# When ScalarE scales du * B: another division of its pieces over the steps of a selective scan

## The chip, the cores and the metric

The kernel runs on one core of a Trainium2 chip, in one launch. The metric is the device time of that launch in microseconds (us), the median of several runs. In what follows TensorE is PE in the profile, VectorE is DVE, ScalarE is ACT, GpSimd is POOL, and SP is the queue that issues the DMAs.

## What is computed

The reference is a small network in four layers on an image of shape 4 x 64 x 64 x 96. Layers 0 and 1 are state-space blocks (projection, depthwise convolution, SiLU, a selective scan in four directions, a normalisation, a gate and a projection; layer 1 works between a Fourier transform and its inverse). Layers 2 and 3 are attention and feed-forward layers. Nearly all of the time goes to the selective scans. For each direction, channel d and state n of 16:

```python
dA = jnp.exp(dl[..., None] * A)
hst = hst * dA + (dl * ul)[..., None] * bl[:, :, None, :]
y = jnp.einsum('bkdn,bkn->bkd', hst, cl)
```

`dl` is delta, a softplus of a projection; `ul` is the input; `bl` and `cl` are the B and C of that time step. The product `du = dl * ul` times `bl` is the "du * B" of this document.

## The kernel before

**Segments and steps.** The scans are cut into segments of up to 512 time steps. Block l0 (layer 0) has two image pairs, four directions and eight segments of 512: 64 segments, with two images side by side on the partitions (`NI` is 2). Block l1 (layer 1) has four images, four directions and segments of 512, 512, 384, 384 and 320: 80 segments, `NI` is 1. A segment is worked off in 12 steps: four quarters q of the 16 states, and in each of them three chunks c of 128 channels. A step (q, c) handles four states of one chunk. The steps run (0,0), (0,1), (0,2), (1,0) and so on to (3,2); there are 1728 of them.

**One step.** VectorE runs four scan instructions (line 643): two for the first two states (the tile hx), two for the others (hy), and then one multiply with C (line 807, the tile hcy). Each scan needs its exp(delta * A), made by ScalarE (line 618), and its du * B:

- For the hx pair, du * B is made on ScalarE in time-major layout, in `make_bx` (line 593), and transposed by TensorE into PSUM (line 613). One call of `make_bx` makes the two states of a quarter for all three chunks. It consists of 16 pieces in l0 (two states, four blocks of 128 time steps, two images; 128x192 each), and in l1 of 8 pieces for 512 time steps or 6 for 384 and 320 (128x384 each). It is a generator: each `next` issues one piece. This document calls the 6 to 16 pieces of one call a set.
- For the hy pair, du * B is made by GpSimd (line 636). Only the exp stands in PSUM.

The exps of the hy pair and the transposed hx products share a ring of three PSUM buffers (the tag `ab`; in the trace the names ab, b and a shortened _l). So an exp can be written only after the scan that used the buffer before has ended. ScalarE's order in a step is: exp of the fourth scan (`front_y(st, 1)`, which follows the first scan), two exps for the next step (`front_x(nxt)`), a burst if one is due, copies of the side work (`slot`), the first share of pieces, again a slot, the copy of the end state (which follows the fourth scan), the exp of the next step's third scan (`front_y(nxt, 0)`), the second share of pieces, the copies of finished outputs, and a last slot. Every engine keeps the written order.

**Bursts.** A burst is a long piece of ScalarE's work that needs another activation table: softplus for the delta of the next segment (line 537, between two table loads), or SiLU in a side task (lines 284 and 345). `burst()` issues it in the first half of a step and returns true; the step is then called `long`. In a long step the end state is copied by GpSimd instead of ScalarE. 185 of the 1728 steps are long: softplus lies at (1,2) in all 143 segments that prepare a next one, and SiLU in 42 other steps.

**The division of the pieces.** A set for quarter q+2 begins at the step c = 2 of quarter q (for q of 0 and 1), the set for the next segment's quarter 0 at (3,0), and the one for its quarter 1 at (3,2). `per` is a third of the pieces of 512 time steps, rounded up: 6 in l0, 3 in l1. A step issues half of `per` (rounded up) as its first share and the rest as its second. In a long step the first share is empty, and all of `per` comes as the second. What is left of a set at the next step with c = 2 is issued at once by `drain(bgen)` there, ahead of the transposes for the next step. The set that begins at (3,0) has only the two steps (3,0) and (3,1) before this drain.

**Side work.** Tasks of other layers and images run in the slots of the same loop, as does the preparation of the next segment (`prepare`). The copies that empty their PSUM buffers are deferred to the next slot.

The lines that the following speaks of: 593 (pieces), 598 (`take`), 613 (transposes), 618 (exps), 636 (GpSimd's product), 643 (scans), 770 (`per`), 777 (`burst`), 782 (`drain`), 791, 792 and 801 (the two shares).

Of the kernel before, what the change touches and what calls it, by code (L numbers as in the profile page):

```python
# [21 lines left out]
C, P = 3, 128  # L22
# [7 lines left out]
class Cfg:  # L30
# [5 lines left out]
    def __init__(self, pre, NI, KI, NR, nat, R, parts, rows, segs, eps):  # L36
        self.pre = pre
        self.NI, self.PI, self.KI = NI, P // NI, KI
        self.DI = C * self.PI
        self.NR, self.L, self.nat = NR, NR * 64, nat  # L40
        self.R, self.M = R, R + 2 * NST
        self.parts = parts
        self.rows = [(sum(rows[:i]), n) for i, n in enumerate(rows)]
        self.segs = [(sum(segs[:i]), n) for i, n in enumerate(segs)]
        self.eps = eps
# [427 lines left out]
def scans(tc, ctx, phases, ident):  # L473
# [9 lines left out]
    NBK = SM // P  # L483
# [5 lines left out]
    segs = []  # L489
# [89 lines left out]
    def fetch(z, q):  # L579
        z.c[q] = [broadcast(z, 4 * q + 2 * j, 1) for j in range(2)]  # L580
        z.b[q] = broadcast(z, 4 * q + 2, 0)

    def make_bx(z, q):

        NI, PI, M, R = z.cfg.NI, z.cfg.PI, z.cfg.M, z.cfg.R
        for j in range(2):
            t = sp.tile([P, NBK, C, P], F32, name=f"bx_{z.nm}_{q}_{j}", tag="bx", bufs=4)
            z.bx[q, j] = t
            for b, (_, n) in enumerate(z.blocks):
                for i in range(NI):  # L590
                    m = i * M + R + 4 * q + j
                    ch = slice(i * PI, (i + 1) * PI)
                    nc.scalar.activation(  # L593
                        t[:n, b, :, ch], z.dut[:n, b, :, ch], AF.Copy, scale=z.bt[:n, b, m : m + 1]
                    )
                    yield

    def take(gen, n):
        for _ in range(n):
            next(gen, None)  # L600

    def drain(gen):
        for _ in gen:
            pass
# [4 lines left out]
    def transposed(st, j):  # L609

        pb = room(st, j)
        for b, (t, n) in enumerate(st.z.blocks):
            nc.tensor.transpose(pb[:, t : t + n], st.z.bx[st.q, j][:n, b, st.c], ident[:n, :n])  # L613
        return pb
# [7 lines left out]
    def front_x(st):  # L622
        st.ax = sp.tile([P, 2, SM], F32, name=f"ax_{st.nm}", tag="ax", bufs=2)
        for j in range(2):
            exp(st.ax[:, j, : st.z.S], st, 4 * st.q + j)

    def front_y(st, j):
        st.ay[j] = room(st, 2 + j)
        exp(st.ay[j][:, : st.z.S], st, 4 * st.q + 2 + j)

    def front_b(st):

        S = st.z.S
        st.hy = sp.tile([P, 2, SM], F32, name=f"hy_{st.nm}", tag="hy")
        for j in range(2):
            nc.gpsimd.tensor_tensor(  # L636
                st.hy[:, j, :S], st.z.du[:, st.c, :S], st.z.b[st.q][:, j, :S], ALU.mult
            )
# [48 lines left out]
    def close_chunk(st):  # L687

        z, c = st.z, st.c
        y = sp.tile([P, NBK, P], F32, name=f"y_{st.nm}", tag="y", bufs=2)  # L690
        for lo, hi, n in z.runs:
            nc.scalar.copy(y[:n, lo:hi], z.acc[c][:n, lo:hi])
            t = z.a + lo * P
            nc.sync.dma_start(
                out=z.ph.io["y"][z.k % 2][z.k // 2, t : t + (hi - lo) * n, c * P : (c + 1) * P].rearrange(
                    "(b p) d -> p b d", p=n
                ),
                in_=y[:n, lo:hi],
            )

    steps = [Step(z, q, c) for z in segs for q in range(NQ) for c in range(C)]
    none = iter(())
    with tc.manual_schedule(engines=IN_ORDER):
        drain(prepare(segs[0]))
        drain(make_bx(segs[0], 0))
        fetch(segs[0], 0)
        st = steps[0]
        st.px, st.ay = [transposed(st, j) for j in range(2)], {}
        front_x(st)
        front_b(st)  # L710
        front_y(st, 0)
        closing = None
        bgen, pgen, pwants, at, due = make_bx(segs[0], 1), none, None, 0, 0.0

        def prepare_more(kind):

            nonlocal pwants
            if pwants not in (None, kind):
                return False
            pwants = next(pgen, LATE)  # L720
            return True

        def slot(kind, hold=False):


            nonlocal due
            if hold:
                E.flush()
                return
            prepare_more(kind)  # L730
            due = min(due + st.z.ph.rate / 3, 3.0)
            if due >= 1.0:
                due -= E.step(kind)

        def burst():

            if BURST in (pwants, E.wants):
                E.flush()
            if pwants is BURST:
                return prepare_more(BURST)  # L740
            if E.wants is BURST:
                E.step(BURST)
                return True
            return False

        for i, st in enumerate(steps):
            z, q, c, S = st.z, st.q, st.c, st.z.S
            nxt = steps[i + 1] if i + 1 < len(steps) else None
            if q == 0 and c == 0:
                after = z.after  # L750
                if at == 0 or z.ph is not segs[at - 1].ph:
                    if closing:
                        close_chunk(closing)
                        closing = None
                    z.ph.io["y"] = [z.blk.dram_tile(f"y{j}", (2, z.cfg.L, C * P), z.ph.g) for j in range(2)]
                    for fn, arg in z.ph.side:
                        E.add((fn, arg), fn(E, arg))
                open_segment(z, segs[at - 1] if at else None)
                if after:
                    E.require(after.ph.needs[after.k % 2])  # L760
                pgen, pwants = prepare(after) if after else none, None
                at += 1
            if c == 0:
                if q + 1 < NQ:
                    fetch(z, q + 1)
                elif after:
                    drain(pgen)
                    bgen = make_bx(after, 0)
                    fetch(after, 0)
            per = -(-2 * z.cfg.NI * NBK // C)  # L770
            hx = sp.tile([P, 2, SM], F32, name=f"hx_{st.nm}", tag="hx")
            scan(st, hx, 0, st.ax[:, 0], st.px[0], 4 * q)
            front_y(st, 1)
            if nxt:
                nxt.ay = {}
                front_x(nxt)
            long = burst()
            scan(st, hx, 1, st.ax[:, 1], st.px[1], 4 * q + 1)
            slot(None)
            if nxt:  # L780
                if c == C - 1:
                    drain(bgen)
                    if q + 2 < NQ:
                        bgen = make_bx(z, q + 2)
                    elif q + 1 == NQ:
                        bgen = make_bx(nxt.z, 1)
                nxt.px = [transposed(nxt, 0)]
            hcx = sp.tile([P, 2, SM], F32, name=f"hcx_{st.nm}", tag="hcx", bufs=2)
            nc.gpsimd.tensor_tensor(hcx[:, :, :S], hx[:, :, :S], z.c[q][0][:, :, :S], ALU.mult)  # L789
            keep_state(nc.gpsimd.tensor_copy, st, hx, 4 * q)  # L790
            first = 0 if long else per - per // 2
            take(bgen, first)
            scan(st, st.hy, 0, st.ay[0], st.hy[:, 0], 4 * q + 2)
            if nxt:
                nxt.px.append(transposed(nxt, 1))
            slot(None, hold=long)
            scan(st, st.hy, 1, st.ay[1], st.hy[:, 1], 4 * q + 3)
            keep_state(nc.gpsimd.tensor_copy if long else nc.scalar.copy, st, st.hy, 4 * q + 2)
            if nxt:
                front_y(nxt, 0)  # L800
            take(bgen, per - first)
            if closing:
                close_chunk(closing)
            accumulate(st, hcx, 4 * q)
            slot(LATE)
            hcy = sp.tile([P, 2, SM], F32, name=f"hcy_{st.nm}", tag="hcy", bufs=2)
            nc.vector.tensor_tensor(hcy[:, :, :S], st.hy[:, :, :S], z.c[q][1][:, :, :S], ALU.mult)  # L807
            if nxt:
                front_b(nxt)
            accumulate(st, hcy, 4 * q + 2)  # L810
            closing = st if q == NQ - 1 else None
        close_chunk(closing)
        E.finish()
# [588 lines left out]
```

## Time and profile before

| what | us |
|---|---|
| median of 3 runs (12100.39 to 12110.57) | 12104.8 |
| the profiled execution | 12108.82 |
| span of the profiled execution, first to last instruction | 12106.9 |
| PE busy | 9441.0 |
| ScalarE: pieces of du * B, line 593, 6272 instructions | 2771.7 |
| VectorE: multiply for du, line 553, 144 instructions | 264.8 |

Rows of the profile name a line, an engine and an operation, then output and input tiles with their buffer numbers left out. In the list of waits, the three numbers are the total in us, how often, and the longest. In the timeline, the first two numbers are the start after the span's begin and the duration, both in us; equal instructions that follow each other are merged with a count (x6), and the brackets give the idle time of the engine just ahead and what ended it. Neighbouring instructions of ScalarE overlap a little in the records.

### The profile page before, as it was taken

Reading aid. Unit: us, or ns where it says so; the run is one execution under the profiler, and the core shown is the slowest. Engines: PE = TensorE matmul, PEld = TensorE weight load, DVE = VectorE, ACT = ScalarE, POOL = GpSimd, SP = SyncE. Lnnn points to the kernel's source line nnn. Section 1 sums busy time; section 2 is a strip of 40 time slices with the busy share of each in tenths; the row PEclk is TensorE's granted clock in tenths of the full one; section 3 lists DMA queues with packets and bytes.
Section 4 is the critical chain, followed back from the end, with each engine's and each line's share of the span. In section 5 each row is a group of like instructions: output and inputs, shape, how many; then the busy total and the mean of one; then the engine's idle time right before and its main releaser. Section 6 shows DMA issues by size and latency. Waiting matters only on the chain. (4 is left out here: it accounts for less than half of the span.)

```text
span 12106.9 us, 164888 instructions
## 1 busy us (share of the span) xinstructions
PE 9441.0 (78%) x54800; PEld 6783.4 (56%) x54800; DVE 10572.7 (87%) x10183; ACT 9071.5 (75%) x18534; POOL 8900.0 (74%) x7074
## 2 busy tenths in 40 slices
PE   5677777777788778777888888788778877887765
PEld 2455555555666556556665565565556555565544
DVE  6899999999999999998879888988989899899854
ACT  3778888898778888887667777777777677777733
POOL 2888889888778888987668877877667766676630
PEclk8889999989889989998879889888878877898886
DMA  5554444556555445445543443444224422452231
GB/s 142 123 135 115 119 125 112 134 157 158 146 143 117 129 130 128 129 132 154 144 120 112 130 123 116 152 128 115 85 91 145 118 82 88 135 132 89 82 103 36
DMA packets 1270447, 1469.07 MB, mean 121 GB/s; under 512 B 496023, under 2 KB 1033823, under 8 KB 1260119
## 3 DMA queue, kind: packets, MB, share of 16 engines
q1 hardware_dynamic: 1269591, 1458.53, 44.1%
q8 instruction: 431, 7.06, 0.2%
q14 instruction: 425, 3.48, 0.1%
HBM read 1221.74 MB, written 236.50 MB: 120 GB/s over the span
## 5 line engine op out<-in xcount | busy, mean ns | idle before, releaser
L636 POOL TENSOR_TENSOR hy_l<-du_l,bc_l 128x512 f32<-128x512 f32 (+2 forms) x3456 | 3956.4, 1165 | 2266.6 <-DVE hcy_l L807 1206.7
L789 POOL TENSOR_TENSOR hcx_l<-hx_l,bc_l 128x1024 f32<-128x1024 f32 (+2 forms) x1616 | 3524.5, 2181 | 279.6 <-DVE hx_l L643 244.1
L593 ACT ACTIVATE bx_l<-dut_l,bt_l 128x192 f32<-128x192 f32 (+2 forms) x6272 | 2771.7, 498 | 0.1
L665 PE MATMUL acc_l<-ident,hcx_l 128*128 128x128 f32 (+1 forms) x12000 | 1885.7, 306 | 357.1 <-POOL hcx_l L789 353.3
L665 PE MATMUL acc_l<-ident,hcy_l 128*128 128x128 f32 (+1 forms) x11994 | 1850.5, 302 | 381.9 <-DVE hcy_l L807 378.5
L618 ACT ACTIVATE ax_l<-delta_l,l_alog 128x512 f32<-128x512 f32 (+2 forms) x3456 | 2139.3, 667 | 0.0
L665 PEld LDWEIGHTS acc_l<-ident,hcy_l 128*128 128x128 f32 (+1 forms) x11994 | 1550.1, 156 | 945.6 <-DVE hcy_l L807 571.3
L665 PEld LDWEIGHTS acc_l<-ident,hcx_l 128*128 128x128 f32 (+1 forms) x12000 | 1545.3, 157 | 852.5 <-POOL hcx_l L789 615.0
L807 DVE TENSOR_TENSOR hcy_l<-hy_l,bc_l 128x1024 f32<-128x1024 f32 (+2 forms) x1615 | 1950.7, 1208 | 43.0
L643 DVE TENSOR_TENSOR_SCAN hx_l<-ax_l,state_l,b_l 128x512 f32<-128x512 f32 (+2 forms) x1648 | 1786.8, 1125 | 222.8 <-PE b_l L613 142.1
L643 DVE TENSOR_TENSOR_SCAN hy_l<-b_l,state_l,hy_l 128x512 f32<-128x512 f32 (+2 forms) x1648 | 1789.7, 1121 | 143.8 <-ACT b_l L618 122.4
L618 ACT ACTIVATE b_l<-delta_l,l_alog 128x512 f32<-128x512 f32 (+2 forms) x1912 | 1200.4, 628 | 881.4 <-DVE hx_l L643 839.3
L613 PE MATMUL b_l<-ident,bx_l 128*128 128x128 f32 (+1 forms) x6718 | 1184.5, 303 | 408.3 <-DVE hy_l L643 193.5
L618 ACT ACTIVATE ab_l<-delta_l,l_alog 128x512 f32<-128x512 f32 x1321 | 909.3, 688 | 700.3 <-DVE hx_l L643 668.7
L613 PEld LDWEIGHTS b_l<-ident,bx_l 128*128 128x128 f32 (+1 forms) x6718 | 825.8, 152 | 905.8 <-DVE hy_l L643 296.7
L643 DVE TENSOR_TENSOR_SCAN hy_l<-ab_l,state_l,hy_l 128x512 f32<-128x512 f32 x961 | 1177.1, 1260 | 97.0 <-ACT ab_l L618 62.0
L643 DVE TENSOR_TENSOR_SCAN hx_l<-ax_l,state_l,ab_l 128x512 f32<-128x512 f32 x962 | 1177.5, 1265 | 95.6 <-PE ab_l L613 66.3
L613 PE MATMUL ab_l<-ident,bx_l 128*128 128x128 f32 x5288 | 903.3, 306 | 454.2 <-DVE hy_l L643 218.0
L656 POOL COPY state_l<-hx_l 128x2 f32<-128x2 f32 x1344 | 1114.3, 829 | 0.0
L613 PEld LDWEIGHTS ab_l<-ident,bx_l 128*128 128x128 f32 x5288 | 653.5, 154 | 799.4 <-DVE hy_l L643 298.5
L272 PE MATMUL pc_l<-pad_l,l_dg 128*128 128x512 f32 (+2 forms) x1656 | 796.5, 569 | 77.9 <-ACT uh_l L250 72.2
L176 PE MATMUL pi_l<-xi_l,l_wi 96*128 96x384 f32 (+6 forms) x912 | 469.0, 629 | 248.2 <-DMA xi_l<-xn 94.8
(193 smaller groups left out, 11970.2 us busy)
## 6 DMA issues: line engine op xcount, KB each, us to landing
bc_l<-l_xd_l SPq DMA_DIRECT2D x1536, 256.0 KB
bc_l<-l_xd_l SPq DMA_DIRECT2D x384, 512.0 KB
bc_l<-l_xd_l SPq DMA_DIRECT2D x384, 384.0 KB
us_l<-l_u SPq DMA_DIRECT2D x96, 768.0 KB
l_y<-y_l SPq DMA_DIRECT2D x288, 256.0 KB
bc_l<-l_xd_l SPq DMA_DIRECT2D x192, 320.0 KB
yt_l<-l_y SPq DMA_DIRECT2D x264, 192.0 KB
yt_l<-l_y SPq DMA_DIRECT2D x128, 384.0 KB
```

The costliest lines, as they stand in the source:

```text
L176: self.nc.tensor.matmul(out[i * cfg.PI : (i + 1) * cfg.PI, :n], wi[:, ki, half, :], xin[:, max(i, ki), :n], start=(ki == 0), stop=(ki == c ...
L272: nc.tensor.matmul(pc[:, : n * 64].rearrange("p (r w) -> p r w", w=64), diag[:, t, :], pad[:, r - p0 + dy : r - p0 + dy + n, dx : dx + 64] ...
L593: nc.scalar.activation(t[:n, b, :, ch], z.dut[:n, b, :, ch], AF.Copy, scale=z.bt[:n, b, m : m + 1])
L613: nc.tensor.transpose(pb[:, t : t + n], st.z.bx[st.q, j][:n, b, st.c], ident[:n, :n])
L618: nc.scalar.activation(out, z.delta[:, st.c, : z.S], AF.Exp, scale=z.blk.A[:, st.c, z.k, n : n + 1])
L636: nc.gpsimd.tensor_tensor(st.hy[:, j, :S], st.z.du[:, st.c, :S], st.z.b[st.q][:, j, :S], ALU.mult)
L643: nc.vector.tensor_tensor_scan(h[:, j, : z.S][:, ::step], a[:, : z.S][:, ::step], b[:, : z.S][:, ::step], 0.0 if z.first else z.state[st.c ...
L656: copy(z.state[st.c][:, n0 : n0 + 2].rearrange("p (j o) -> p j o", o=1), h[:, :, e : e + 1])
L665: nc.tensor.matmul(z.acc[st.c][:n, b, :], hc[:, j, t : t + n], ident, start=(n0 + j == 0 and b == 0), stop=(n0 + j == NST - 1 and b == 0), ...
L789: nc.gpsimd.tensor_tensor(hcx[:, :, :S], hx[:, :, :S], z.c[q][0][:, :, :S], ALU.mult)
L807: nc.vector.tensor_tensor(hcy[:, :, :S], st.hy[:, :, :S], z.c[q][1][:, :, :S], ALU.mult)
```

## The change

A class `Pieces` takes the place of `take` and `per`. It knows how many pieces of a set are left and how many half-steps remain until the drain, and each half-step issues the quotient, rounded up. Sets that begin at c = 2 have six half-steps, the set that begins at (3,0) and the very first one have four. The first half of a long step issues nothing, as before. The second half of a long step now issues its share, except where c is 2: there it issues nothing, and the four half-steps left take all of the set.

```diff
-    def take(gen, n):
-        for _ in range(n):
-            next(gen, None)
+    class Pieces:
+        def __init__(self, z, q, halves):
+            self.gen, self.halves = make_bx(z, q), halves
+            self.left = 2 * z.cfg.NI * len(z.blocks)
+
+        def take(self, skip=False):
+            n = 0 if skip else -(-self.left // max(self.halves, 1))
+            self.halves -= 1
+            self.left -= n
+            for _ in range(n):
+                next(self.gen, None)
...
-        bgen, pgen, pwants, at, due = make_bx(segs[0], 1), none, None, 0, 0.0
+        more, pgen, pwants, at, due = Pieces(segs[0], 1, 4), none, None, 0, 0.0
...
-                    bgen = make_bx(after, 0)
+                    more = Pieces(after, 0, 4)
...
-            per = -(-2 * z.cfg.NI * NBK // C)
...
-                    drain(bgen)
+                    drain(more.gen)
                     if q + 2 < NQ:
-                        bgen = make_bx(z, q + 2)
+                        more = Pieces(z, q + 2, 6)
                     elif q + 1 == NQ:
-                        bgen = make_bx(nxt.z, 1)
+                        more = Pieces(nxt.z, 1, 6)
...
-            first = 0 if long else per - per // 2
-            take(bgen, first)
+            more.take(skip=long)
...
-            take(bgen, per - first)
+            more.take(skip=long and c == C - 1)
```

The pieces per half-step in the usual segment, by their order in the two programs (step: first + second share, and what the drain issues):

| steps | l0 before | l0 after | l1, 512 before | l1, 512 after |
|---|---|---|---|---|
| (0,2), (1,0), (1,1) | 3+3, 3+3, 3+1 | 3+3, 3+3, 2+2 | 2+1, 2+1, 2+0 | 2+2, 1+1, 1+1 |
| (1,2) long, (2,0), (2,1) | 0+6, 3+3, 3+1 | 0+0, 4+4, 4+4 | 0+3, 2+1, 2+0 | 0+0, 2+2, 2+2 |
| (3,0), (3,1), drain at (3,2) | 3+3, 3+3, 4 | 4+4, 4+4, 0 | 2+1, 2+1, 2 | 2+2, 2+2, 0 |

Before, a long (3,2) issued its drain of 4 and then 0+6 in l0; after, it issues none.

## The prediction

> **What bounds the kernel now.** First the page's busy shares: VectorE is the fullest engine, ScalarE has a quarter of the span free.
>
> ```profile
> PE 9441.0 (78%) x54800; PEld 6783.4 (56%) x54800; DVE 10572.7 (87%) x10183; ACT 9071.5 (75%) x18534; POOL 8900.0 (74%) x7074
> ```
>
> So a change of order on ScalarE can only pay where VectorE stands idle for it. The second view is the list of who waited for whom, VectorE's rows (total us, times, longest).
>
> ```profile
> DVE hx_l L643 <- PE b_l L613: 166.8, 97, 7.6
> ...
> DVE hy_l L643 <- ACT b_l L618: 141.9, 143, 3.9
> DVE hx_l L643 <- PE ab_l L613: 119.4, 53, 9.4
> ...
> DVE hy_l L643 <- ACT ab_l L618: 86.6, 85, 4.0
> ```
>
> The hy scans wait for ScalarE's exps of line 618 (b and ab are the ring of PSUM buffers that holds them). To place these waits I numbered the 6912 scans of the trace, four to a step, (q, c) being quarter and channel chunk, and took the idle time ahead of each scan. The fourth scan (hy, j=1) waits 225.6 us in all, and 118.1 us of it stand in 143 steps: those at (2,0), right behind the step (1,2) with softplus between its table loads. One of them in the timeline, ScalarE and then VectorE:
>
> ```profile
> 2149.48 1.28 ACT L538 ACT_TABLE_LOAD   x1
> 2150.77 0.69 ACT L618 ACTIVATE b_l<-delta_l,l_alog 128x512 f32<-128x512 f32 x1
> 2151.40 2.17 ACT L593 ACTIVATE bx_l<-dut_l,bt_l 128x192 f32<-128x192 f32 x6
> 2153.47 0.67 ACT L618 ACTIVATE b_l<-delta_l,l_alog 128x512 f32<-128x512 f32 x1
> ```
>
> ```profile
> 2148.81 2.44 DVE L643 TENSOR_TENSOR_SCAN hx_l<-ax_l,state_l,b_l 128x512 f32<-128x512 f32 x2
> 2151.57 1.28 DVE L643 TENSOR_TENSOR_SCAN hy_l<-b_l,state_l,hy_l 128x512 f32<-128x512 f32 x1 [0.32 <-ACT b_l L618]
> 2154.25 1.28 DVE L643 TENSOR_TENSOR_SCAN hy_l<-b_l,state_l,hy_l 128x512 f32<-128x512 f32 x1 [1.40 <-ACT b_l L618]
> ```
>
> Six pieces of du * B (line 593) run between the two exps; the second exp is late by them, and VectorE loses 1.40 us. The other place is the drain at (3,2) when a side task's SiLU falls into that step:
>
> ```profile
> 2189.04 1.28 ACT L286 ACT_TABLE_LOAD   x1
> 2190.33 1.49 ACT L593 ACTIVATE bx_l<-dut_l,bt_l 128x192 f32<-128x192 f32 x4
> 2191.73 0.67 ACT L618 ACTIVATE b_l<-delta_l,l_alog 128x512 f32<-128x512 f32 x1
> ```
>
> ```profile
> 2192.39 1.22 DVE L643 TENSOR_TENSOR_SCAN hx_l<-ax_l,b_l 128x512 f32<-128x512 f32 x1 [2.90 <-PE b_l L613]
> 2193.53 1.20 DVE L643 TENSOR_TENSOR_SCAN hy_l<-b_l,hy_l 128x512 f32<-128x512 f32 x1
> 2195.67 1.22 DVE L643 TENSOR_TENSOR_SCAN hy_l<-b_l,hy_l 128x512 f32<-128x512 f32 x1 [0.95 <-ACT b_l L618]
> ```
>
> The four drained pieces feed the transposes for the next hx scan, so that scan waits 2.90 us for TensorE. Eight such cases make 20.6 us, nearly all the waiting of the second scan.
>
> [...] the exp of 2153.47 starts only as the sixth piece ends, though its buffer was free at 2150.05. [...] Piece to piece the starts lie 0.346 us apart at a duration of 0.442 (128x192), and 0.506 at 0.603 (128x384)[...]. So I charge 0.346 and 0.506 per piece, not the durations.
>
> **The change part by part.** Counts are read from the order of ScalarE's instructions in both programs; 6272 pieces either way, nothing else moves on any engine.
>
> *Pieces behind softplus.* In the 143 steps (1,2) pieces fall from 6 to 0 (64 steps of block l0) or 3 to 0 (79 of l1). ScalarE's queue loses 6 x 0.346 = 2.08 us or 3 x 0.506 = 1.52 us ahead of the late exp. The waits there, each cut at what is removed: 65.4 (l0), 12.7, 25.9 and 13.0 (l1 with 512, 384, 320 columns): 117.0 of 118.1. GpSimd's product for that scan would still be ready about 1.2 us ahead on average in l0, 1.5 to 2.3 in l1, once the wait is taken off, so it isn't next. What stays is the hy scan before it, waiting for the exp straight behind the burst (0.32 above): 32.2 us in these steps, untouched.
>
> *Pieces behind SiLU.* 42 more steps hold a burst. In 14 all pieces leave: 19.8 us of fourth-scan wait and the 20.6 us of second-scan wait. Where 2.90 us of the latter goes, the exp behind the burst becomes the next late one, about 0.3 us in 8 cases as at 2151.57: 2.5 us back. Net 37.9. In 5 some pieces leave (two each, 3.3 us off), in 12 nothing changes, in 9 more pieces come: 21 in all, 21 x 0.37 = 8 us at most, 5 taken because two of these steps lie under the multiply at (2,1).
>
> *Where they go.* In l0, (2,0) gets 8 for 6, (2,1) 8 for 4, (3,0) 8 for 6, (3,1) 8 for 6, and (3,2) loses its drain of 4. ScalarE's occupied time per step (exp to exp, less its idle) goes from 5.08, 4.30, 5.02, 5.47, 6.72 to 5.77, 5.68, 5.71, 6.16, 5.34; VectorE's own work in these steps (duration less idle) is 6.22, 7.85, 6.13, 6.14, 6.2. (2,1) holds the multiply for du (1.88 us) and hides its four. Only (3,1) touches the limit, by 0.02. Within a step two more pieces delay the exp at most 0.69 us, and its slack is 1.4 us on average at (2,1), (3,1), (3,2). Today 1, 1 and 4 of the 144 steps at these places wait for ScalarE without a burst ahead. I charge 6 x 0.7 + 8 more x 0.5 = 8 us. The bounds: nothing, or 0.35 us in all 128 l0 steps at (3,1) and (3,2), 45 us. Below nothing: 13 late steps at (0,0), behind the old drain, may recover up to 10.
>
> *In l1*, over the six half-steps of a set, pieces go from 2,1,2,1,2,0 to 2,2,1,1,1,1 (512 columns) and from 2,1,2,1,0,0 to six ones (384 and 320); steps that had none idle 2.2 to 2.5 us on ScalarE, so 2 x 0.506 costs nothing there. Without that cover it would be 1.01 us in some 96 steps. In the 384 and 320 segments q=3 gets 2,2,1,1 for 2,1,2,1, also covered.
>
> *What takes over.* 10% of the 155 us is charged, 15.5 us, to TensorE and GpSimd having less time to catch up: hx scans wait 286 us for TensorE today. The bounds of this are 0 and half, 77.
>
> *Sum.* 117.0 + 37.9 + 3.3 - 5 - 8 - 15.5 = 129.7, say 130 us. The profiled execution took 12108.8 us, 2 of them around its span of 12106.9; the median of the runs is 4 lower. 12108.8 - 130 - 4 = 11975 us.
>
> **Rivals.**
>
> *Half of it moves to another wait.* With the exp in time, the product from GpSimd or the transposes come next. For it: GpSimd is 74% busy, its margin ahead of the fourth scan is about 1 us in ordinary steps. Against: the two steps that follow have ScalarE and GpSimd idle under VectorE's du multiply. Gain 65: 12040 us.
>
> *Side copies held back, slower.* Copies that empty PSUM for the side tasks and for the next segment sit in the slots behind the pieces; the second slot now comes one piece later (0.35 us), the last one two to four later (0.7 to 1.4) in the four l0 steps with 8 pieces. TensorE's queue is in order, and its next matmul into the single buffer waits for the copy, with the transposes for the next hx scan behind it. Against: the copies have until the next slot, about 2 us. It decides from 155 / 256 = 0.6 us lost in each of the 256 steps; at 0.7 it takes 179 and gives 12105 + 24 = 12129 us.
>
> *It does not do what it says, or nothing gains.* The counts exclude the first; the second would need the fourth scan to be held by something else at the same moment, as the 9 waits put down to GpSimd's state copy (12.2 us) might say. In the one I looked at, the scan starts at 1434.58 and ScalarE's exp ends at 1434.48, so the exp is its cause too. 12105 us.
>
> **How the numbers follow.** Own case 0.68, half 0.15, nothing 0.06, slower 0.11. The own case reaches from 11920 (no takeover, no knock-on, the 10 at (0,0), and some relief where l1's pieces are now even) to 12020 (45 of knock-on). With most of the half case, the range is 11920 to 12050. 0.2% is 24 us, about what a measurement of this kernel tells from no change; faster than 12081 takes the own case, the half case, in sum 0.82 with rounding; same 0.07; slower 0.11.
>
> **What would show it.** Right: the fourth scan's waits at (2,0) fall from 118 us to under 20, the second scan's from 20.7 to under 3, no row of pieces between softplus's second load and the second exp. Wrong: hy waits for ScalarE appear at (3,1), (3,2), or hx waits for TensorE grow past 286 us by over 60.

## The result and the profile after

The changed kernel took 11910.4 us (median of four runs, 11891.7 to 11917.7), the kernel before 12102.6 us beside it: a ratio of 0.984, with an interval from 0.982 to 0.986. It is faster by 192 us. The forecast was 130 us; the direction was right, and the time lies 10 us below the lower end of the range. In two more pairs the same text gained 185 us and 170 us (below), so the gain to be explained is about 180.

The page of the changed kernel, its span and its busy times:

```profile
span 11915.9 us, 164932 instructions
...
PE 9346.5 (78%) x54800; PEld 6707.9 (56%) x54800; DVE 10559.1 (89%) x10183; ACT 9087.2 (76%) x18534; POOL 8930.4 (75%) x7074
```

Each engine has as many counted instructions as before. VectorE's busy time fell by 14 us only, but the span by 191: what went is VectorE's idle time. The list of who waited for whom (total us, times, longest) says for whom it no longer waits; the scans now stand on line 653, the exps on 628 and the transposes on 623:

```profile
DVE hx_l L653 <- PE b_l L623: 172.0, 98, 7.8
...
DVE hx_l L653 <- PE ab_l L623: 103.7, 42, 7.9
...
DVE hy_l L653 <- ACT b_l L628: 87.2, 92, 4.2
...
DVE hy_l L653 <- ACT ab_l L628: 38.9, 40, 4.2
```

The two hy rows fell from 228.5 us to 126.1. The two hx rows, where the prediction feared the time would turn up again, hold 275.7 us after 286.2. This is the same step (2,0) that the prediction showed, ScalarE first (start, duration, then the instruction; brackets give the idle time just ahead):

```profile
2123.65 1.28 ACT L538 ACT_TABLE_LOAD   x1
2124.95 1.30 ACT L628 ACTIVATE b_l<-delta_l,l_alog 128x512 f32<-128x512 f32 x2
2126.19 1.32 ACT L628 ACTIVATE ax_l<-delta_l,l_alog 128x512 f32<-128x512 f32 x2
2127.42 0.39 ACT L548 COPY bt_l<-pp_l 128x304 f32<-128x304 f32 x1
2127.71 1.49 ACT L593 ACTIVATE bx_l<-dut_l,bt_l 128x192 f32<-128x192 f32 x4
```

```profile
2122.98 2.44 DVE L653 TENSOR_TENSOR_SCAN hx_l<-ax_l,state_l,b_l 128x512 f32<-128x512 f32 x2
2125.74 2.46 DVE L653 TENSOR_TENSOR_SCAN hy_l<-b_l,state_l,hy_l 128x512 f32<-128x512 f32 x2 [0.32 <-ACT b_l L628]
2128.23 1.23 DVE L815 TENSOR_TENSOR hcy_l<-hy_l,bc_l 128x1024 f32<-128x1024 f32 x1
```

The two exps behind the second table load now stand next to each other. The third scan still waits 0.32 us for the first of them, as it did; the fourth follows without a wait. The four pieces of the new share start at 2127.71, behind all the exps that these scans and the next two need. This is the second place, a step (0,0) behind a SiLU in (3,2), with no drained pieces between the load and the exp, ScalarE and then VectorE:

```profile
2162.07 1.28 ACT L286 ACT_TABLE_LOAD   x1
2163.37 0.69 ACT L628 ACTIVATE b_l<-delta_l,l_alog 128x512 f32<-128x512 f32 x1
```

```profile
2160.96 2.32 DVE L653 TENSOR_TENSOR_SCAN hx_l<-ax_l,b_l 128x512 f32<-128x512 f32 x2
2164.16 2.34 DVE L653 TENSOR_TENSOR_SCAN hy_l<-b_l,hy_l 128x512 f32<-128x512 f32 x2 [0.88 <-ACT b_l L628]
```

The second hx scan has no wait. The exp behind the burst is the next late one, as foreseen, and costs 0.88 us here.

To compare whole kernels, I numbered the scans of each trace as in the prediction, four to a step, and added up the idle time ahead of each. All in us; "loop" is the time from the first step's first scan to the last step's:

| kernel | loop | fourth scan at (2,0) | second scan, all steps | fourth scan behind the other 42 bursts | VectorE's time in the loop outside its waits |
|---|---|---|---|---|---|
| before, the first profile | 11422.0 | 118.1 | 20.7 | 61.2 | 10310.8 |
| before, a second profile | 11390.5 | 117.9 | 21.0 | 59.7 | 10311.2 |
| changed | 11228.0 | 1.1 | 0.0 | 48.9 | 10297.1 |
| changed, a second profile | 11231.4 | 1.1 | 0.3 | 47.3 | 10297.1 |

Two profiles of the same text before differ by 31 us in the loop and agree to 2 us in each wait that the change touches. So a single profile is good for a tally of certain waits, and less good for what lies in the other steps: 24 of the 31 us stand there, in steps without a burst ahead.

### The profile page after: what moved, and what is told of

Same layout as the page of the kernel before. It is cut to its first block, busy times and chain, and to the rows that moved or that the text cites. A ratio compares the mean times of both kernels' runs of the same rounds, so it can differ in the third digit from the quotient of the medians.

```text
span 11915.9 us, 164932 instructions
## 1 busy us (share of the span) xinstructions
PE 9346.5 (78%) x54800; PEld 6707.9 (56%) x54800; DVE 10559.1 (89%) x10183; ACT 9087.2 (76%) x18534; POOL 8930.4 (75%) x7074
## 5 line engine op out<-in xcount | busy, mean ns | idle before, releaser
L675 PE MATMUL acc_l<-ident,hcx_l 128*128 128x128 f32 (+1 forms) x12000 | 1845.4, 301 | 392.8 <-POOL hcx_l L798 387.7
L675 PEld LDWEIGHTS acc_l<-ident,hcx_l 128*128 128x128 f32 (+1 forms) x12000 | 1505.6, 154 | 885.6 <-POOL hcx_l L798 667.9
L623 PE MATMUL ab_l<-ident,bx_l 128*128 128x128 f32 x5288 | 878.0, 301 | 414.5 <-DVE hy_l L653 227.4
L666 POOL COPY state_l<-hx_l 128x2 f32<-128x2 f32 x1344 | 1140.2, 848 | 0.0
```

Source lines behind the costliest of these rows:

```text
L666: copy(z.state[st.c][:, n0 : n0 + 2].rearrange("p (j o) -> p j o", o=1), h[:, :, e : e + 1])
L675: nc.tensor.matmul(z.acc[st.c][:n, b, :], hc[:, j, t : t + n], ident, start=(n0 + j == 0 and b == 0), stop=(n0 + j == NST - 1 and b == 0), ...
```

## The experiments

Open after the result: whether the direct terms are as large as summed, what the reserve for "What takes over" stood for, whether the even shares have a worth of their own, and whether the surprise is partly a high profile of before (theory S in the expectation for the repeat). All runs below came in three groups, each timed beside the kernel before on one chip; its median was 12096.2, 12093.6 and 12095.9 us there. The texts speak of theory P (the waits give back nine tenths), A (they give back their length and something more) and E (the rest comes from the even shares).

**Only the pieces behind bursts.** The shares of before, and the drain, are kept. A set that begins in a long step with c = 2 issues nothing there and is spread over the next four half-steps:

```diff
-            take(bgen, per - first)
+            more.take(long, True, c)
...
+            if long and c == C - 1:
+                self.even = True
+                n = 0
+            elif self.even:
+                n = 0 if long and not second else -(-self.left // max(self.halves, 1))
```

> The kernel before with one part of the change: a long step with c = 2 issues no piece of the set begun there, and the four half-steps after it share the set evenly. All other sets keep the old shares, and the drain at (3,2) keeps its 4 pieces in l0. The waits of the fourth scan that this can remove are 117.0 us behind softplus and about 20 us behind SiLU at (0,2) and (3,2). Theory P (the sum of the prediction: a wait gives back nine tenths of its length): 118 us less than before, ratio 0.990. Theory A (a removed wait gives back its length, about 0.1 us more for each wait, and shorter waits of the work that runs late behind it): 150 to 180 us less, ratio 0.986. Theory E (the gain beyond the prediction comes from the even shares elsewhere): 118 us less, as P.

Measured: 11925.4 us, ratio 0.9856 (0.9842 to 0.9869), 171 us less than before, within what theory A gave. The fourth scan at (2,0) waits 1.4 us in all, and the second scan still 22.7, which belongs to the drain that this kernel keeps. The same (0,0) as above, ScalarE and then VectorE, where the scans stand on line 664 and the exps on 639:

```profile
2166.98 1.28 ACT L286 ACT_TABLE_LOAD   x1
2168.27 1.49 ACT L593 ACTIVATE bx_l<-dut_l,bt_l 128x192 f32<-128x192 f32 x4
2169.67 0.67 ACT L639 ACTIVATE b_l<-delta_l,l_alog 128x512 f32<-128x512 f32 x1
```

```profile
2166.21 1.21 DVE L664 TENSOR_TENSOR_SCAN hx_l<-ax_l,b_l 128x512 f32<-128x512 f32 x1
2170.33 1.22 DVE L664 TENSOR_TENSOR_SCAN hx_l<-ax_l,b_l 128x512 f32<-128x512 f32 x1 [2.91 <-PE b_l L634]
```

The four drained pieces stand between load and exp again, and the scan waits 2.91 us, put down to TensorE. TensorE itself could not transpose before the pieces were there; in the kernel before, at the same place, its row reads

```profile
2191.18 0.48 PE L613 MATMUL b_l<-ident,bx_l 128*128 128x128 f32 x1 [4.71 <-ACT bx_l L593]
```

What follows: this part alone is most of the gain, and more than the waits that it removes, 117 us at (2,0) and 13 behind other bursts. Not all of that surplus is shown to be its own. In its profile, beside the mean of the two of before, the steps at (2,0) are 126 us shorter and those behind the other bursts 14; another 21 us lie in the steps without a burst ahead, where the two profiles of before differ by 24.

**Only the drain.** The set that begins at (3,0) is shared out evenly, so that (3,2) has nothing to drain; all other sets are as before, six pieces behind softplus included:

```diff
+            self.per, self.even = -(-2 * z.cfg.NI * NBK // C), halves == 4
...
+            if self.even:
+                n = 0 if long and not second else -(-self.left // max(self.halves, 1))
```

> The kernel before with another part: only the set begun at (3,0) is shared evenly over its four half-steps (4 and 4 for 3 and 3 in l0), so that nothing is left for the drain at (3,2). Six pieces stay behind softplus. It removes the 20.6 us of the second scan's waits and adds pieces at (3,0) and (3,1). Theory P: 8 us less than before, ratio 0.999. Theory A: 10 to 20 us less. Theory E: up to 30 us less. In the profile the second scan's waits should be near 0 under all three.

Measured: 12067.7 us, 0.9972 (0.9962 to 0.9982), 29 us less, the upper end of what theory E gave. The second scan's waits are gone (0.5 us in all), the fourth scan at (2,0) keeps its 118.5. The drain's removal does not return the 20.7 us whole: in the eight steps (0,0) where it stood behind a SiLU, six pieces (three in l1) still run behind that burst, so part of the wait moves to the scans after it, and the steps (0,0) behind bursts get 12 us shorter. The other steps (0,0) get 23 us shorter, of which VectorE's own work is 8, most of it in the multiply hcy, and first scans that wait less are some 10. So the drain cost something in steps without a burst too; how much of these 10 would come again wasn't tried.

**Only the even shares.** Sets with six half-steps are shared evenly, but a long step with c = 2 issues all of `per` as before, and the drain stays:

```diff
+            self.per, self.even = -(-2 * z.cfg.NI * NBK // C), halves == 6
...
+            if self.even and long and c == C - 1:
+                n = self.per if second else 0
+            elif self.even:
+                n = 0 if long and not second else -(-self.left // max(self.halves, 1))
```

> The kernel before with the rest of the change: sets with six half-steps are shared evenly (2 and 2 for 3 and 1 at c = 1 in l0; 1 and 1 for 2 and 1 and for 0 and 0 in l1), but a long step with c = 2 still issues 6 (3 in l1) behind its burst, and the set begun at (3,0) keeps its old shares and its drain. Theories P and A: within 10 us of before. Theory E: 40 to 60 us less, ratio 0.995 to 0.997.

Measured: 12072.7 us, 0.998 (0.9972 to 0.9988), 24 us less, which none of the theories gave. Since the prediction had put this at nothing, the same text was run again:

> The even shares alone once more. The first time they were 24 us under before by the medians, while the loop of the profile was level with the repeat of the kernel before. If the even shares have a worth of their own: again 14 to 34 us under before. If not: within 10 us.

Measured: 12075.3 us, 0.9981 (0.9971 to 0.999), 21 us less. So the even shares are worth some 22 us of their own. In both traces the first scans wait less for ScalarE (85.4 and 85.6 us against 93.7 and 95.8), and VectorE's time outside waits is 8 us shorter, half of it in l1's steps (2,1), where the multiply for du is shorter. Why that multiply is shorter wasn't tried.

**More pieces behind softplus.** The other way round, to measure the slope: in the kernel before, 10 pieces instead of 6 in l0 and 5 instead of 3 in l1.

```diff
-            take(bgen, per - first)
+            take(bgen, per - first + (2 * z.cfg.NI if long and q == 1 and c == C - 1 else 0))
```

> The kernel before with the suspected cost raised: 10 pieces instead of 6 behind softplus in l0 and 5 instead of 3 in l1, taken from the steps after. The late exp moves by 4 x 0.346 = 1.38 us in 64 segments and by 2 x 0.506 = 1.01 us in 79, or less where there was no wait yet. By the waits of the kernel before, the fourth scan's wait at (2,0) grows by about 84 us in l0 and 68 us in l1, 152 in all. Theory P: 137 us more than before (nine tenths). Theory A: the waits already exist, so the 0.1 us for each is paid already and the slope is near 1 unless the late work behind pays again: 152 us, up to 190 if it does.

Measured: 12223.3 us, 1.0101 (1.0085 to 1.0116), 127 us more: nearest to theory P's 137, and below the 152 to 190 of theory A, which had fitted the removal. The same place as above, ScalarE and then VectorE:

```profile
2177.29 1.28 ACT L538 ACT_TABLE_LOAD   x1
2178.58 0.69 ACT L618 ACTIVATE b_l<-delta_l,l_alog 128x512 f32<-128x512 f32 x1
2179.21 3.55 ACT L593 ACTIVATE bx_l<-dut_l,bt_l 128x192 f32<-128x192 f32 x10
2182.66 0.67 ACT L618 ACTIVATE b_l<-delta_l,l_alog 128x512 f32<-128x512 f32 x1
```

```profile
2176.63 2.44 DVE L643 TENSOR_TENSOR_SCAN hx_l<-ax_l,state_l,b_l 128x512 f32<-128x512 f32 x2
2179.37 1.28 DVE L643 TENSOR_TENSOR_SCAN hy_l<-b_l,state_l,hy_l 128x512 f32<-128x512 f32 x1 [0.30 <-POOL hy_l L636]
2183.44 1.28 DVE L643 TENSOR_TENSOR_SCAN hy_l<-b_l,state_l,hy_l 128x512 f32<-128x512 f32 x1 [2.78 <-ACT b_l L618]
```

Four pieces more are 4 x 0.346 = 1.38 us, and the wait grew from 1.40 to 2.78, by just that. Over all the fourth scan at (2,0) waits 264.2 us, 146 more. That is also read off the rows of the hy scans in the list of waits:

```profile
DVE hy_l L643 <- ACT b_l L618: 230.7, 151, 3.5
...
DVE hy_l L643 <- ACT ab_l L618: 132.1, 86, 4.2
```

The sum of the two is 362.8 us, 134 above the kernel before. The price per piece and its place on the path are thus shown from both sides. But the added wait comes without an extra of its own: the steps at (2,0) are 140 us longer than the mean of the two profiles of before, for 146 us of wait, and the side instructions there wait no longer for ScalarE than before (19.2 us after 19.1). So what removal gained beyond the wait has no counterpart here.

**Repeats.** The two kernels once more, as a control and for theory S:

> The kernel before, unchanged, once more: it shows how far two profiles and two medians of one text lie apart. In four other kernels the steps that no part of their edits touches stood 16 to 33 us below the profile of before. Theory S (that profile was a slow one of its kind; the rest differs from execution to execution): the untouched steps here are again 10 to 25 us below it, ratio 1.000. Theory C (the changed order of the pieces itself relieves them): they stand within 5 us of that profile.

Measured: 12089.4 us, 0.9997 (0.9989 to 1.0006). Its loop is the 11390.5 of the table: the profile that the prediction worked from was a high one by 31 us, 24 of it in the steps without a burst ahead, as theory S said.

> The changed kernel, unchanged, on the same chip as the others of this call. By the parts (171 + 29 + 24 = 224 us less than before) it should be 224 us under before if they add; by its first timing 192 us. In the profile the steps at (2,0) and behind other bursts should again be 169 us shorter than before, and 15 to 25 us more come from the rest.

Measured: 11908.4 us, 0.9845 (0.9832 to 0.9858), 185 us less, not the 224 of the parts added up.

> The changed kernel once more, as the base for the next two on one chip. Expected 185 to 192 us under before, and in the profile the same two places: near 1 us of the fourth scan's waits at (2,0), side work's waits there near 31 us.

Measured: 11925.8 us (11893.2 to 11932.2), 0.9855 (0.984 to 0.9869), 170 us less, below what was expected. The gain of the change is known to some 10 us either way, not better.

**A version beyond the change.** What ScalarE still does late in the changed kernel is seen at (3,0). There `drain(pgen)` issues the rest of the preparation of the next segment ahead of the step's first exp. ScalarE and VectorE of the changed kernel in such a step:

```profile
10221.31 0.53 ACT L564 COPY dut_l<-pp_l 128x256 f32<-128x256 f32 x2 [2.25 <-PE pp_l L561]
10224.00 0.53 ACT L564 COPY dut_l<-pp_l 128x256 f32<-128x256 f32 x2 [2.17 <-PE pp_l L561]
10224.43 0.58 ACT L628 ACTIVATE b_l<-delta_l,l_alog 128x384 f32<-128x384 f32 x1
```

```profile
10220.13 1.92 DVE L653 TENSOR_TENSOR_SCAN hx_l<-ax_l,state_l,b_l 128x384 f32<-128x384 f32 x2 [0.74 <-PE b_l L623]
10221.96 0.99 DVE L653 TENSOR_TENSOR_SCAN hy_l<-b_l,state_l,hy_l 128x384 f32<-128x384 f32 x1
10225.11 1.02 DVE L653 TENSOR_TENSOR_SCAN hy_l<-b_l,state_l,hy_l 128x384 f32<-128x384 f32 x1 [2.16 <-ACT b_l L628]
```

The exp that the fourth scan needs stands behind copies which wait for TensorE: ScalarE is idle 2.17 us, and VectorE loses 2.16. The edit to the changed kernel moves that drain to just ahead of the first share of pieces, behind the exps:

```diff
-                    drain(pgen)
                     more = Pieces(after, 0, 4)
...
+            if after and q == NQ - 1 and c == 0:
+                drain(pgen)
             more.take(skip=long)
```

> The changed kernel with one more move: at (3,0) the last copies of the next segment's preparation come behind the three exps instead of ahead of them. The fourth scan at (3,0) waits about 30 us in the changed kernel for the exp behind these copies. If it is ScalarE's order alone that costs: 15 to 30 us less than the changed kernel. If the copies only move the wait to the pieces and to TensorE's transposes: no change.

Measured: 11892.6 us, 0.9837 (0.9823 to 0.9852), 16 us below the repeat of the changed kernel in the same group. The same step, ScalarE and VectorE:

```profile
10199.72 0.53 ACT L564 COPY dut_l<-pp_l 128x256 f32<-128x256 f32 x2 [2.25 <-PE pp_l L561]
10200.15 0.58 ACT L628 ACTIVATE b_l<-delta_l,l_alog 128x384 f32<-128x384 f32 x1
10200.66 1.11 ACT L628 ACTIVATE ax_l<-delta_l,l_alog 128x384 f32<-128x384 f32 x2
10202.40 0.53 ACT L564 COPY dut_l<-pp_l 128x256 f32<-128x256 f32 x2 [0.62 <-PE pp_l L561]
```

```profile
10198.54 1.92 DVE L653 TENSOR_TENSOR_SCAN hx_l<-ax_l,state_l,b_l 128x384 f32<-128x384 f32 x2 [0.75 <-PE b_l L623]
10200.38 1.90 DVE L653 TENSOR_TENSOR_SCAN hy_l<-b_l,state_l,hy_l 128x384 f32<-128x384 f32 x2
```

The exp now precedes the second pair of copies, and the two hy scans run without a gap. Over all steps (3,0) the fourth scan's waits go from 32.8 us to 1.0. Once more, beside the third run of the changed kernel:

> The changed kernel with the later copies at (3,0) once more. The first pair showed 16 us less in the medians, with intervals that overlap, and 31 us less of the fourth scan's waits at (3,0). If that is a gain of the order on ScalarE: again 10 to 30 us less than the changed kernel. If it was chance: within 8 us.

Measured: 11897.9 us, 0.9837 (0.9824 to 0.985), 28 us below it, with 1.1 us of waits at (3,0) against 25.3. The wait is gone in both traces and the median lower in both pairs, but each pair's intervals overlap: a gain of the size of the removed wait is likely, and not proven by the times alone.

On top of it, a long step with c = 0 also issued no second share, outside the last quarter:

```diff
-            more.take(skip=long and c == C - 1)
+            more.take(skip=long and (c == C - 1 or (c == 0 and q + 1 < NQ)))
```

> The kernel with the later drain, and besides a long step with c = 0 (q under 3) issues no pieces behind its burst either; that concerns about 9 steps with a wait of 12 us together. By the waits: 8 to 12 us less than with the later drain alone, which may be too little to tell.

Measured: 11892.3 us, 0.9833 (0.9819 to 0.9846); against the 11892.6 without this edit no difference can be told. In the trace the fourth scan's waits behind the 42 other bursts do fall, from 39.9 us to 31.3, but the loop is as long as in the two profiles without the edit (11207.5 us; 11204.3 and 11207.4). A wait of this size that goes need not show in the time.

## What of the prediction held, and which step of it failed

The account of the loop, the mean of the two profiles of before against the mean of three of the changed kernel, in us saved:

| term of the prediction | forecast | measured |
|---|---|---|
| pieces behind softplus: the fourth scan at (2,0) | 117.0 | 116.9 |
| pieces behind SiLU (37.9 + 3.3 - 5); measured as the length of the 42 steps behind these bursts | 36.2 | 35.3 |
| where they go: forecast for (3,1) and (3,2); measured over all steps without a burst ahead | -8 | +7.4, in it -6.1 for the fourth scan at (3,1) and (3,2) |
| what takes over; measured as all else that changed in the steps at (2,0) | -15.5 | +14.8 |
| sum (rounded) | 129.7 | 174.5 |

**The direct terms were right.** 153.2 us were summed and 152.2 measured. The price per piece, the distance from start to start (0.346 and 0.506 us) and not the duration (0.442 and 0.603), is confirmed twice: by the kernel with more pieces behind softplus, and by what stays. Only two waits at (2,0) were longer than the three l1 pieces ahead of them (2.07 us against 3 x 0.506 = 1.52), and these two keep 0.55 us each, the 1.1 us of the table. In the second term the closeness is in part luck. Its waits fell by 34 us in the 14 steps where all pieces leave (37.9 forecast) and by 4 where some do (3.3), and grew by 8 where more come (5); the 14 steps whose pieces stay the same wait 3 us less. The prediction names 12 of these 14 (its counts add up to 40 of the 42 bursts; the other two, at (2,2), have no pieces in either kernel). The order of the late ones was right: the hy scan behind the burst keeps its wait (0.32 us in the step shown), and where the second scan's 2.90 us go the exp is next (0.88 us in the step shown, 0.3 foreseen).

**The step that failed is "What takes over".** It charged 10% of the 155 us to TensorE and GpSimd having less time to catch up, and set the bounds of this at nothing and at half. Neither bound lies below nothing. In the traces nothing took over: the hx scans' waits for TensorE, where the test line was 286 plus 60, are 275.7, 251.3 and 279.6 us in three profiles of the changed kernel, 286.2 and 273.2 before. What came was of the other sign: 14.8 us more saved at (2,0) where 15.5 were charged. That is 30 of the 45 us by which the forecast fell short; the steps without a burst ahead give the other 15. VectorE's side instructions wait 61.2 to 63.7 us for ScalarE in the changed kernel, 76.9 and 77.8 before. At (2,0) their waits are 10 us less, 7 of it for ScalarE and 3 for TensorE; the other scans there and VectorE's own work give 5 more. The kernel with only that part has nearly as much: at (2,0) its steps are 126 us shorter for 117 us of wait. A likely reason, argued and not tested by itself: with the pieces out of ScalarE's queue, everything behind them comes earlier, not the exp alone. In l0 ScalarE's queue loses 2.08 us there and VectorE's mean wait was 1.02, so by this estimate ScalarE gets ahead by the difference. Where pieces are added to a wait that exists, both are held up alike, and then no extra comes, as was measured (140 us for 146 us of wait). A charge for knock-on wants a bound on each side: the price of less slack downstream, and the gain of work that was queued behind the same obstacle.

**The even shares are a second step that was mis-sized: costed at nothing, they bring some 22 us,** in two runs whose intervals lie below 1. "Costs nothing there" was right about the cost; the relief entered only as a remark at the edge of the range. Which wait pays it could not be told: the parts visible are 9 us of first-scan waits and 8 us of VectorE's work. In the changed kernel, too, the steps without a burst ahead are 7 us shorter in all where 8 were charged, with VectorE's own work there 12 us shorter; that the drain and the even shares bring this is what their two kernels suggest.

**The parts do not add up.** Alone they gain 171, 29 and 22 us, 222 in sum; the whole gains 170 to 192. In the loops of the profiles it is 161, 27 and 17 us, 206 in sum (the two profiles of the even shares averaged), against 174.5. Of the 31 us between, 4 are counted twice: VectorE's own work in l1's (2,1) gets 5 us shorter with the first part alone, 4 with the even shares alone, and 5 in the whole. The rest is no more than what two profiles of one text differ by. By the medians the gap is 30 to 52 us, and it stays open.

**Knock-on at (3,1) and (3,2)** was sized well: 22.5 us of fourth-scan waits became 27.5 to 29.2.

**The rivals.** Half of it moving to another wait would have shown as a growth of the hx or GpSimd rows; there is none beyond what two profiles of one text differ by. Side copies held back do occur: at one place in the trace of before, TensorE is idle for 4.41 us ahead of a matmul of a side task (line 176), which starts at 6352.36 as a copy on ScalarE (line 234) ends; the transposes behind it start at 6353.80, though both hy scans of the step had ended by 6351.75, and the next hx scan waits 1.98 us. But the rival would have needed 0.6 us lost in each of 256 steps; VectorE's side work waits some 15 us less for ScalarE instead. That nothing gains is excluded by 192 us. What was to show the prediction right did: 1.1 us at (2,0) where under 20 was asked, at most 0.3 us of second-scan waits where under 3 was asked, no pieces between the second load and the second exp.

## What to carry to other kernels

Count what stands in an engine's queue between a long piece of work and the first instruction that another engine waits for. In the trace of before, the scans and multiplies of VectorE, the products of GpSimd (lines 636 and 789) and the exps of ScalarE stand in the written order in all 1728 steps, and the late exp of the prediction starts 3.42 us after its buffer was free, as the pieces ahead of it end. Here three or six small instructions, which could have run anywhere in the next two steps, made VectorE wait 118 us at 143 places, and with them moved all but 1 us of that wait is gone. Look then at what else stands behind the same obstacle, since it may come earlier too (14.8 us more were saved at (2,0), for the reason argued above), and give the estimate of side effects a bound on both sides of nothing. The same reading finds the next case: copies that wait for a third engine ahead of an exp that VectorE needs (2.16 us of wait in the step shown).

## What the runs showed of the hardware

**A wait cost more than its idle time.** In the trace of before, a 512-column hy scan in l0 that follows the scan before it without a wait starts 1.17 us behind it (mean of 655 fourth scans), though each lasts 1.25 us in the records; where it waits (98 of them), its start stands 1.26 us behind once the idle time is taken off. So the scans overlap by 0.08 us where nothing holds them, and a wait loses about 0.09 besides its idle time. In l0's (2,0) the hy scans occupy 161.7 us of VectorE before and 155.4 after (128 scans).

**VectorE's multiply took longer where GpSimd was busy.** The gain just named was given back in the same steps: the 1024-column multiplies hcy of l0's (2,0) last 1.27 us on average before and 1.35 after. Before, GpSimd is busy during 7% of their time, after during 54%. Over all 1152 multiplies of this size in the trace of before, the mean is 1.22 us with GpSimd busy for under 5% of it (294 of them) and 1.36 with GpSimd busy throughout (623). This is a correlation within the traces (spans on GpSimd are rough); no run was made for it alone. VectorE moved up, in these steps, to where GpSimd was busier, and the 14 us that it saves of its own work over the loop are a balance of such terms.

**A table load took 1.28 us, and no wait ahead of it shows.** The 144 loads of line 537 last 1283 ns each in the trace of before, with 2.6 us of ScalarE's idle time ahead of all of them together.

**TensorE stood at half clock for longer where VectorE stalled more.** In the records of the granted clock, half clock takes some 2810 and 2725 us of the loop before, 2515 to 2560 in the three profiles of the changed kernel, and 2975 with more pieces behind softplus; the mean granted clock of these profiles is 0.870 and 0.872, 0.878 to 0.880, and 0.865. In l0's (2,1), the step after the stall, the loss of clock is 14%, 20% and 33% with none, 6 and 10 pieces behind softplus, where the fourth scan at (2,0) waits 1.1, 118.1 and 264.2 us over all 143 steps. That the two go together is what these runs show; by which path wasn't tried. It isn't seen in the time: the hx scans' waits for TensorE show no such order (251.3 to 279.6 us in the changed kernel, 286.2 and 273.2 before, 272.2 with more pieces).
